# A fixed order for the beginning of the first attention in a two-layer decoder kernel

## The chip, the cores and the metric

The kernel runs on one core of a Trainium2 chip. The metric is the time of one execution on the device in microseconds (us); the median of several runs counts.

## The reference

Two decoder layers in float32 on x of 8 sequences x 512 tokens x 256 channels. Only the first attention matters here; behind it come a feed-forward layer, a second attention over another axis, and a mixture of 32 experts.

```
x = x + L0_attn(layernorm(x));  x = x + L0_ffn(layernorm(x))
x = x + L1_attn(layernorm(x));  x = x + L1_experts(layernorm(x))

L0_attn(h):                                   # 16 heads of 16 channels
  q, k, v = split_heads(h@Wq+bq), split_heads(h@Wk+bk), split_heads(h@Wv+bv)
  scores  = q.k / sqrt(48)
  pos_k   = rel_embeddings @ Wk + bk          # 128 relative positions per head
  c2p     = take(q.pos_k, bucket(i - j) + 64) # by query and distance
  p2c     = take(k.pos_k, 64 - bucket(j - i)) # by key and distance, turned
  probs   = softmax(scores + (c2p + p2c)/sqrt(48))
  return layernorm((probs.v) @ Wo + bo + h)
```

## The kernel before, in words

All tensors lie in tiles of 128 partitions. The five engines run their own queues in order; semaphores tie them. The code is written for a scheduler that may reorder what stands outside a `manual_schedule` block, and inside it keeps the written order, except that an instruction with nothing to wait for can be moved forward on its engine.

The first attention (`_l0_attention`) has three parts.

**The beginning** prepares constants. DMAs bring the weights `wk`, `wq`, `wv`, the table `relT`, bias rows, one-hot tables `oh`, and the sequences x[0] to x[7]; all but four are issued by SP, in one queue. Four scratch buffers in DRAM (`shift`, 1 MB each) are filled with zeros from the tile `zeros`. VectorE (DVE) normalises x[0] (L47 to L63: statistics, variance, a power on POOL, then one subtract-and-multiply per 128 tokens). `position_keys` (L170) makes relative keys with TensorE, adds the bias on DVE, once for all positions (`pk`) and twice for an end position broadcast (`end0`, `end1`). From `pk` and `oh` eight matmuls (L190) make the tables `posc` and `posp`. From the ends come 12 products on POOL (L205, L208), each reduced on DVE (L206, L209) into extra columns of `wq`, `wk` and the bias rows; ACT copies the bias rows (L213), POOL sets a column in each copy (L214), and 16 matmuls with one column (L217) make `bias`. POOL clears two `v` tiles (L233) and four `winc` tiles (L240). `turn` (L264) transposes normalised x[0] into `xnT`; `project` (L283) makes q and k of one group of four heads with TensorE (L291) and ACT adds the bias (L299) in four tiles `sm`.

**The strips** (L307). Scores with relative positions need each row shifted by its own index. For step u = (sequence, group, row block i, pair of heads p), TensorE multiplies q and k by the position tables (L315), ACT copies the result out (L322, `strip`), SP writes it to a `shift` buffer in DRAM (L332), and reads it back with a row step that is one element shorter (L341): once into `winp` (to be transposed later) and once into `winc`. POOL makes the part of the far positions (`own`, L325) and adds it (L352). Reads of a strip are issued after the write of the next one, additions after the strip after that. Five strips (AHEAD) are made before the first step, with the values of the first sequence (L273) between them.

**The steps**, 256 of them: TensorE makes scores (L372), with the strip five steps ahead in their midst, adds `winp` by transposing it into the same bank (L384; it needs the windows of up to two steps ahead), DVE adds `winc` and finds the maximum (L398), ACT takes the exponential (L401), TensorE transposes (L412), DVE copies (L415), TensorE weighs the values (L424). Projections and other work of the next group hang on given steps. Only the strips and steps stand in a `manual_schedule` block; the beginning is ordered by the scheduler.

Of the kernel before, what the change touches and what calls it, by code (L numbers as in the profile page):

```python
# [12 lines left out]
F32 = mybir.dt.float32  # L13
# [3 lines left out]
ALU = mybir.AluOpType  # L17
# [9 lines left out]
NG = 4  # L27
# [63 lines left out]
def _l0_attention(nc, tc, a, x, ident, mhalf, carry, prefetch):  # L91
# [6 lines left out]
    with ExitStack() as ctx:  # L98
# [16 lines left out]
        bias = wp.tile([P, 4, NG], F32, tag="bias", name="bias")  # L115
        xns = [carry.tile([P, NT, H], F32, tag=f"xn{n}", name=f"xn{n}") for n in range(3)]
        xnT = carry.tile([P, NK, S], F32, tag="xnT0", name="xnT")
        shift = [dram.tile([4 * P, 2 * W], F32, tag=f"shift{n}", name=f"shift{n}") for n in range(NSHIFT)]
        with tc.tile_pool(name="a_pos", bufs=1) as pp:
            b_rows = {n: pp.tile([P, NH, 32], F32, tag=n, name=n) for n in ("bq", "bk")}  # L120
# [16 lines left out]
            aside = wp.tile([P, 2, P], F32, tag="aside", name="aside")  # L137
            nc.sync.dma_start(aside[:, 0, :], a["later"])
            nc.sync.dma_start(aside[:, 1, :], a["earlier"])
            zeros = pp.tile([P, 2 * W], F32, tag="zeros", name="zeros")  # L140
            nc.gpsimd.memset(zeros, 0.0)
            for d in shift:
                nc.sync.dma_start(
                    d.rearrange("(q p) w -> p q w", p=P), zeros.unsqueeze(1).to_broadcast([P, 4, 2 * W])
                )
            nc.sync.dma_start(wo, a["wo_rows"].rearrange("(g p) m -> p g m", p=P))
            for name in ("bo", "ln_scale", "ln_bias"):
                nc.sync.dma_start(rows[name], a[name].partition_broadcast(P))
            for b in range(1, B):
                nc.sync.dma_start(x[b], a["x"][b].rearrange("(t p) c -> p t c", p=P))  # L150

            def normalized(pool, b):

# [9 lines left out]
                return [partial(f, t) for f in (measure, norm) for t in (0, 2)]  # L163

            ready = normalized(pp, 0)
            for n in (0, 2, 1, 3):
                ready[n]()


            def position_keys(lhsT, out):  # L170
                ps = ps_m.tile([P, S], F32, tag="misc", name="pk_ps")
# [8 lines left out]
            nc.vector.memset(pk, 0.0)  # L180
            position_keys(lambda k: relT[:, k, :], pk[:, :, :HD])
            ends = []
            for n, c in enumerate((P - 1, 0)):
                f = pp.tile([P, NH, HD], F32, tag=f"end{n}", name=f"end{n}")
                position_keys(lambda k: relT[:, k, c : c + 1].to_broadcast([P, P]), f)
                ends.append(f)
            for g in range(NG):
                for t, dst in ((0, posc), (1, posp)):
                    pe = ps_a.tile([P, S], F32, tag="psa", name="pe")
                    nc.tensor.matmul(  # L190
                        pe[:, :W], pk[:, 4 * g : 4 * g + 4, :].rearrange("p h e -> p (h e)"), oh[:, t, :], start=True, stop=True
                    )
                    if t == 0:
                        nc.vector.tensor_copy(dst[:, g, :], pe[:, :W])
                    else:
                        nc.scalar.mul(dst[:, g, :], pe[:, :W], -SCALE)
                    nc.vector.tensor_copy(dst[:, g, W - 1 : W], tail[:, t : t + 1])


            for (w, name), e0 in (((wq, "bq"), HD), ((wk, "bk"), HD + 2)):  # L200
                for n, f in enumerate(ends):
                    e = e0 + n
                    for k in range(NK):
                        prod = pp.tile([P, NH, HD], F32, tag="prod", name="prod", bufs=3)
                        nc.gpsimd.tensor_tensor(prod, w[:, k, :, :HD], f, ALU.mult)  # L205
                        nc.vector.tensor_reduce(w[:, k, :, e : e + 1].rearrange("p h e -> p (h e)"), prod, AX.X, ALU.add)  # L206
                    prod = pp.tile([P, NH, HD], F32, tag="prod", name="prod", bufs=3)
                    nc.gpsimd.tensor_tensor(prod, b_rows[name][:, :, :HD], f, ALU.mult)  # L208
                    nc.vector.tensor_reduce(b_rows[name][:, :, e : e + 1].rearrange("p h e -> p (h e)"), prod, AX.X, ALU.add)  # L209
            pb = ps_m.tile([P, S], F32, tag="misc", name="pb")  # L210
            for n, (name, e) in enumerate((("bq", HD + 2), ("bq", HD + 3), ("bk", HD), ("bk", HD + 1))):
                row = pp.tile([P, NH, 32], F32, tag=f"row{n}", name=f"row{n}")
                nc.scalar.copy(row, b_rows[name])  # L213
                nc.gpsimd.memset(row[:, :, e : e + 1], 1.0)  # L214
                for g in range(NG):
                    c = NG * n + g
                    nc.tensor.matmul(  # L217
                        pb[:, c : c + 1],
                        row[:, 4 * g : 4 * g + 4, :].rearrange("p h e -> p (h e)"),
                        ident[:, 0:1],  # L220
                        start=True,
                        stop=True,
                    )
            flat = bias.rearrange("p n g -> p (n g)")
            nc.vector.tensor_scalar(flat[:, : 2 * NG], pb[:, : 2 * NG], -SCALE, None, ALU.mult)
            nc.vector.tensor_copy(flat[:, 2 * NG :], pb[:, 2 * NG : 4 * NG])

        sb = pool("a_sb", 2)


        vs = [wp.tile([P, NT, 2, NH // 2, 2 * HD], F32, tag=f"v{n}", name=f"v{n}") for n in range(2)]
        for v in vs:
            nc.gpsimd.memset(v, 0.0)  # L233


        winc = [None] * (2 * NT)
        for p in range(2):
            for i, width in ((0, S + 2 * P), (1, S + 3 * P)):
                w = wp.tile([P, 2, width], F32, tag=f"winc{i}{p}", name="winc")
                nc.gpsimd.memset(w, 0.0)  # L240
                winc[2 * i + p], winc[2 * (NT - 1 - i) + p] = w[:, :, :S], w[:, :, width - S :]

        ctx_ps = ps_c.tile([P, S], F32, tag="ctx", name="ctx_ps")
# [9 lines left out]
        reads, adds = [], []  # L253
        cns = {b: [] for b in range(B)}
        rest = []
        now = -1

        def misc(name):

            if now < 0:  # L260
                return ps_t.tile([P, S], F32, tag="pst", name=name)
            return ps_m.tile([P, S], F32, tag="misc", name=name)

        def turn(b, k):  # L264
            pt = misc("pt")
            for t in range(NT):
                nc.tensor.transpose(pt[:, t * P : (t + 1) * P], xns[b % 3][:, t, k * P : (k + 1) * P], ident)
            evac(xnT[:, k, :], pt)

        def values(b, t):  # L270
            pv = misc("pv")
            for k in range(NK):
                nc.tensor.matmul(  # L273
                    pv[:, :H], xnT[:, k, t * P : (t + 1) * P], wv[:, k, :], start=k == 0, stop=k == NK - 1
                )
            by_head = lambda w: w.rearrange("p (h d) -> p h d", d=HD)
            for o in range(2):
                s = slice(o * H // 2, (o + 1) * H // 2)
                nc.vector.tensor_tensor(
                    vs[b % 2][:, t, o, :, HD * o : HD * o + HD], by_head(pv[:, s]), by_head(rows["bv"][:, s]), ALU.add  # L280
                )

        def project(b, g):  # L283


            def half(w, n, scale):
                if n == 0:
                    sm[b, g] = [sb.tile([P, S], F32, tag=f"sm{m}", name=f"sm{m}") for m in range(4)]
                pq = misc("pq")
                for k in range(NK):  # L290
                    nc.tensor.matmul(  # L291
                        pq,
                        w[:, k, 4 * g : 4 * g + 4, :].rearrange("p h e -> p (h e)"),
                        xnT[:, k, :],
                        start=k == 0,
                        stop=k == NK - 1,
                    )
                for m in (n, n + 1):
                    nc.scalar.activation(sm[b, g][m], pq, AF.Identity, bias=bias[:, m, g : g + 1], scale=scale)  # L299

            return [partial(half, wq, 0, -SCALE), partial(half, wk, 2, 1.0)]
# [202 lines left out]


        with tc.manual_schedule():
            for f in [partial(turn, 0, k) for k in range(NK)] + project(0, 0):
                f()
            for u in range(AHEAD):
                strips(u)  # L510
                if u:
                    values(0, u - 1)
            es, ets = None, deque()
            for now in range(len(steps) + 3):
                n = now
# [1169 lines left out]
```

## Time and profile before

| | |
|---|---|
| runs | 2081.64, 2083.9, 2084.47 us; median 2083.9 |
| profiled execution | 2102.91 us, span 2101.1 us |
| mean granted TensorE clock | 0.954 |
| busy share of the span | PE 92%, POOL 54%, DVE 66%, ACT 53% |
| DMA | 444.43 MB, mean 212 GB/s over the span |
| chain that ended last | PE 63%, DVE 11%, DMA 11%, issue 5%, POOL 5%, ACT 3% |
| first strip's write to DRAM issued | 40.46 us from the span's start |
| first score matmul of the steps | 56.49 us |

The profile is one execution on the chip. PE is TensorE, PEld its weight load, SP the queue that issues DMAs. A busy PE is not a PE at its peak: PEclk gives the clock that was granted, 1.00 being full. A matmul in float32 stands as two rows. In the first 7 us the clock column reads 1.00 only because no change of it has been recorded yet; durations of matmuls tell there. DMA share is the mean busy share of 16 DMA engines; small excesses over 1 come from the way packets are counted. In the chain of waits each piece is the work that released the next one; "issue" is time in which the engine waited for nothing that the profile shows.

### The profile page before, as it was taken

How to read it: one execution, taken by the hardware profiler on the slowest of the kernel's cores; microseconds unless marked ns; L12 is line 12 of the kernel's file. 1: busy time of each engine (PE TensorE's matmuls, PEld its weight loads, DVE VectorE, ACT ScalarE, POOL GpSimd, SP SyncE). 2: the span in 40 equal slices, each digit the busy share in tenths (PEclk: the TensorE clock that was granted, in tenths of full speed). 3: DMA queues.
4: the chain of work that ended last, by engine and by line, in shares of the span. 5: the costliest groups of instructions: out<-in, count | busy, mean ns of one | idle time of the engine just before them, and what ended most of it. 6: DMA issues, size and time to landing. Idle time of an engine off the chain costs nothing.

```text
span 2101.1 us, 49496 instructions
## 1 busy us (share of the span) xinstructions
PE 1930.6 (92%) x17956; PEld 1334.9 (64%) x17956; DVE 1389.0 (66%) x3731; ACT 1106.3 (53%) x2366; POOL 1143.3 (54%) x1340
## 2 busy tenths in 40 slices
PE   7999999999999999999889999879888778599997
PEld 4666667666666666676656666545455455388786
DVE  3677777777777777777676454257876775356666
ACT  2677777767777777677631222345433422144443
POOL 4666777767778686776733111114444443455555
PEclk7999999999999999999989999999989987699999
DMA  8999999999999999899944548601111115457888
GB/s 270 305 317 284 310 303 300 292 289 304 295 297 304 296 306 299 286 289 299 285 140 143 167 141 127 20 1 42 42 42 42 42 42 215 169 163 217 256 254 266
DMA packets 388928, 444.43 MB, mean 212 GB/s; under 512 B 43344, under 2 KB 367952, under 8 KB 388688
## 3 DMA queue, kind: packets, MB, share of 16 engines
q1 hardware_dynamic: 373904, 401.93, 63.9%
q0 software_dynamic: 13824, 38.29, 5.0%
q8 instruction: 145, 2.38, 0.5%
q10 hardware_dynamic: 960, 1.05, 0.1%
q14 instruction: 95, 0.78, 0.1%
HBM read 238.99 MB, written 202.19 MB: 210 GB/s over the span
## 4 chain that ended last, share of the span: by engine, by line
PE 63%; DVE 11%; DMA 11%; issue 5%; POOL 5%; ACT 3%; SPq 1%; another core or an unknown queue 0%; POOLq 0%; DVEq 0%; ACTq 0%
PE sc L372 7%; PE sc L384 6%; PE pge L1440 6%; PE et_ps L412 5%; PE po L684 5%; DMA winp<-shift 5%; PE ctx_ps L424 5%; PE pq L291 5%; PE ph L676 3%; PE poe L1458 3%; PE pa L315 3%; DMA shift<-strip 3%; PE pq L935 2%; PE po L460 2%; DVE prod L796 2%
## 5 line engine op out<-in xcount | busy, mean ns | idle before, releaser
L398 DVE CUSTOM_DVE_ANT_0 e<-sc,winc 128x512 f32<-128x512 f32 x512 | 333.3, 689 | 268.1 <-PE sc L384 139.4
L401 ACT ACTIVATE e<-e,low 128x512 f32<-128x512 f32 x512 | 365.7, 715 | 94.8 <-DVE low L398 93.5
L322 ACT COPY strip<-pa 128x512 f32<-128x512 f32 x512 | 275.2, 591 | 138.6 <-POOL winc L352 58.2
L325 POOL TENSOR_TENSOR own<-aside,strip 128x512 f32<-128x512 f32 x256 | 269.1, 1051 | 130.3 <-ACT strip L322 121.6
L415 DVE COPY et<-et_ps 128x512 f32<-128x512 f32 x512 | 328.5, 683 | 0.7 <-PE et_ps L412 0.7
L372 PE MATMUL sc<-sm,sm 32*128 32x256 f32 (+3 forms) x1792 | 310.5, 437 | 0.2
L315 PE MATMUL pa<-pos,sm 32*128 32x256 f32 x2048 | 297.2, 407 | 1.7 <-ACT sm L299 1.0
L879 POOL DMA_INDIRECT rows<-pay,slot x128 | 141.4, 1105 | 237.2 <-issue 224.9
L352 POOL TENSOR_TENSOR winp<-winp,own 128x256 f32<-128x256 f32 x256 | 187.3, 732 | 108.0 <-DMA winp<-shift 78.3
L372 PEld LDWEIGHTS sc<-sm,sm 32*128 32x128 f32 x1792 | 164.1, 184 | 97.0 <-DVE et L415 35.6
L384 PE MATMUL sc<-ident,winp 128*128 128x128 f32 x1280 | 204.9, 287 | 22.4 <-DMA winp<-shift 21.1
L879 POOL DMA_INDIRECT results<-y,r x160 | 157.0, 981 | 124.3 <-ACT y L1460 70.7
L352 POOL TENSOR_TENSOR winc<-winc,own 128x256 f32<-128x256 f32 x256 | 187.2, 731 | 52.2 <-DMA winc<-shift 40.6
L384 PEld LDWEIGHTS sc<-ident,winp 128*128 128x128 f32 x1280 | 137.4, 142 | 102.0 <-issue 58.3
L315 PEld LDWEIGHTS pa<-pos,sm 32*128 32x128 f32 x2048 | 178.5, 187 | 11.5 <-issue 2.0
L412 PE MATMUL et_ps<-ident,e 64*128 64x64 f32 x4096 | 184.2, 230 | 1.1 <-DVE et L415 1.1
L58 POOL TENSOR_TENSOR rstd<-var,mhalf 128x2 f32<-128x2 f32 (+1 forms) x56 | 51.1, 912 | 241.5 <-DVE var L56 208.9
L412 PEld LDWEIGHTS et_ps<-ident,e 64*128 64x128 f32 x4096 | 148.9, 140 | 44.4 <-issue 22.8
L1440 PE MATMUL pge<-store,rT 128*128 x640 | 168.0, 385 | 3.5 <-DVE rT L1434 1.1
L424 PE MATMUL ctx_ps<-et,v 128*32 128x128 f32 x4096 | 166.6, 281 | 0.5 <-DVE et L415 0.5
L291 PE MATMUL pq<-xnT,wqk 128*128 128x512 f32 x256 | 134.0, 646 | 0.1
L679 ACT ACTIVATE hT<-ph,b 128x512 f32<-128x512 f32 x64 | 44.0, 687 | 165.6 <-PE ph L676 165.5
(216 smaller groups left out, 3339.0 us busy)
## 6 DMA issues: line engine op xcount, KB each, us to landing
shift<-strip SPq DMA_DIRECT2D x256, 510.0 KB
winp<-shift SPq DMA_DIRECT2D x128, 384.0 KB
winc<-shift SPq DMA_DIRECT2D x128, 384.0 KB
winp<-shift SPq DMA_DIRECT2D x128, 256.0 KB
winc<-shift SPq DMA_DIRECT2D x128, 256.0 KB
rows<-empty SPq DMA_DIRECT2D x8, 2640.0 KB
r<-rows SPq DMA_DIRECT2D x160, 132.0 KB
z<-results SPq DMA_DIRECT2D x32, 512.0 KB
```

Of the source, the lines that this page charges most:

```text
L315: nc.tensor.matmul(pa[:, t * W : (t + 1) * W], src[rs, i * P : (i + 1) * P], pos[rs, g, :], start=True, stop=True)
L322: nc.scalar.copy(st[:, 2 * j : 2 * j + 2, :].rearrange("p t w -> p (t w)"), pas[j])
L352: nc.gpsimd.tensor_tensor(dst, dst, own[:, t], ALU.add)
L372: nc.tensor.matmul(sc[:, c0:c1], s[side_][rs, cut : cut + P], s[2 + side_][rs, c0:c1], start=c0 == 0, stop=False, skip_group_check=True,)
L384: nc.tensor.matmul(sc[:, m * P : (m + 1) * P], wins[n + 2 * (m - i)][1][:, j, (i - m + 1) * P : (i - m + 2) * P], ident, start=False, stop ...
L398: nc.vector.tensor_tensor_reduce(e, sc, wins[n][0][:, j, :], 1.0, -LOW, ALU.add, ALU.min, low)
L401: nc.scalar.activation(e, e, AF.Exp, bias=low, scale=-1.0, accum_out=totals[b, g // 2][:, i, r : r + 1])
L412: nc.tensor.transpose(bank[:, c : c + 64], e[rs, m * P : (m + 1) * P], ident[rs, rs])
L415: nc.vector.tensor_copy(et[:, f].rearrange("p j m q -> p (j m q)"), bank)
L424: nc.tensor.matmul(ctx_ps[32 * r : 32 * r + 32, i * P : (i + 1) * P], vs[b % 2][:, m, g % 2, g // 2 * 4 + r, :], et[:, :, m, :], start=m = ...
L879: ins = nc.gpsimd.indirect_dma_start(to, bass.IndirectOffsetOnAxis(ap=index, axis=0), source, None, bounds_check=last)
L1440: nc.tensor.matmul(pg[:, :H], rT[:, k * P : (k + 1) * P], w[:, k * H : (k + 1) * H], start=k == 0, stop=k == NK - 1)
```

## The change

It touches the beginning only. In words:

- The beginning is put in a `manual_schedule` block. The two end keys come before `pk`; the 12 products become a generator, `products`, whose pieces are taken between other work; normalising x[0] is taken in four pieces; all eight position tables are copied out by ACT; the constant last column of the tables is written by two DVE instructions instead of eight.
- `busy(n, zeros)` adds n matmuls of zeros by zeros, 128 x 128 by 128 x 512, into a scratch bank that nobody reads: 7 before the first keys, 5 behind `turn`, 4 before the last two bias rows: 16 in all.
- `turn` of x[0] stands before the bias matmuls; both projections of the first group stand after them.
- The six clearings (`v`, `winc`) go from POOL to DVE and stand in the code behind the projections. In the built program they stand earlier: two right after the clearing of `pk`, one after each statistics instruction of the first pair, one before the variance, one between the second and the third keys' additions.
- `zeros` grows from 512 to 2048 columns, and each `shift` buffer is cleared in rows of 8 KB instead of 2 KB. The bytes are the same.
- x[1] is loaded as before; x[2] to x[6] are issued by SP after strips 0 to 4 each, x[7] after the last of them. On SP's queue each such load stands behind a strip's write and the reads of the strip before, and ahead of the next strip's write.

```diff
+        def busy(n, w):
+            idle = misc("idle")
+            for _ in range(n):
+                nc.tensor.matmul(idle, w[:, :P], w[:, :S], start=True, stop=True)
...
-            zeros = pp.tile([P, 2 * W], F32, tag="zeros", name="zeros")
+            zeros = pp.tile([P, 8 * W], F32, tag="zeros", name="zeros")
             nc.gpsimd.memset(zeros, 0.0)
             for d in shift:
-                nc.sync.dma_start(
-                    d.rearrange("(q p) w -> p q w", p=P), zeros.unsqueeze(1).to_broadcast([P, 4, 2 * W])
-                )
+                nc.sync.dma_start(d.rearrange("(p q) w -> p (q w)", p=P), zeros)
...
-            for b in range(1, B):
-                nc.sync.dma_start(x[b], a["x"][b].rearrange("(t p) c -> p t c", p=P))
+            load(1)
...
+            def products():
+                for (w, name), e0 in (((wq, "bq"), HD), ((wk, "bk"), HD + 2)):
+                    for n, f in enumerate(ends):
+                        e = e0 + n
+                        for part in (w[:, 0], w[:, 1], b_rows[name]):
+                            prod = pp.tile([P, NH, HD], F32, tag="prod", name="prod", bufs=4)
+                            nc.gpsimd.tensor_tensor(prod, part[:, :, :HD], f, ALU.mult)
+                            nc.vector.tensor_reduce(
+                                part[:, :, e : e + 1].rearrange("p h e -> p (h e)"), prod, AX.X, ALU.add
+                            )
+                            yield
...
+            with tc.manual_schedule():
+                nc.vector.memset(pk, 0.0)
+                busy(7, zeros)
+                measure[0]()
+                for n, c in enumerate((P - 1, 0)):
+                    f = pp.tile([P, NH, HD], F32, tag=f"end{n}", name=f"end{n}")
+                    position_keys(lambda k: relT[:, k, c : c + 1].to_broadcast([P, P]), f)
+                    ends.append(f)
+                position_keys(lambda k: relT[:, k, :], pk[:, :, :HD])
+                some = products()
+                next(some)
+                norm[0]()
+                next(some)
+                measure[1]()
+                next(some)
+                norm[1]()
+                for g in range(NG):
+                    for t, dst in ((0, posc), (1, posp)):
...
+                        nc.scalar.mul(dst[:, g, :], pe[:, :W], (1.0, -SCALE)[t])
+                for t, dst in ((0, posc), (1, posp)):
+                    nc.vector.tensor_copy(
+                        dst[:, :, W - 1], tail[:, t : t + 1].to_broadcast([P, NG])
+                    )
+                for _ in range(3):
+                    next(some)
+                turn(0, 0)
+                turn(0, 1)
+                busy(5, zeros)
+                bias_columns(0, "bq", HD + 2)
+                bias_columns(1, "bq", HD + 3)
+                for _ in some:
+                    pass
+                busy(4, zeros)
+                bias_columns(2, "bk", HD)
+                bias_columns(3, "bk", HD + 1)
...
-        for v in vs:
-            nc.gpsimd.memset(v, 0.0)
...
-                nc.gpsimd.memset(w, 0.0)
+                cleared.append(w)
...
         with tc.manual_schedule():
-            for f in [partial(turn, 0, k) for k in range(NK)] + project(0, 0):
+            for f in project(0, 0):
                 f()
+            for w in cleared[2:] + cleared[:2]:
+                nc.vector.memset(w, 0.0)
             for u in range(AHEAD):
                 strips(u)
+                load(2 + u)
                 if u:
                     values(0, u - 1)
+            load(7)
```

More of the change, by code (lines that the diff above doesn't have):

```diff
@@ L117, in _l0_attention, with load, misc, turn @@
         xnT = carry.tile([P, NK, S], F32, tag="xnT0", name="xnT")
+        def load(b):
+            nc.sync.dma_start(x[b], a["x"][b].rearrange("(t p) c -> p t c", p=P))
+        def misc(name):
+            if now < 0:
+                return ps_t.tile([P, S], F32, tag="pst", name=name)
+            return ps_m.tile([P, S], F32, tag="misc", name=name)
+        def busy(n, w):
+            idle = misc("idle")
+            for _ in range(n):
+                nc.tensor.matmul(idle, w[:, :P], w[:, :S], start=True, stop=True)
+        def turn(b, k):
+            pt = misc("pt")
+            for t in range(NT):
+                nc.tensor.transpose(pt[:, t * P : (t + 1) * P], xns[b % 3][:, t, k * P : (k + 1) * P], ident)
+            evac(xnT[:, k, :], pt)
+        now = -1
         shift = [dram.tile([4 * P, 2 * W], F32, tag=f"shift{n}", name=f"shift{n}") for n in range(NSHIFT)]
@@ L165, in _l0_attention @@
             ready = normalized(pp, 0)
-            for n in (0, 2, 1, 3):
-                ready[n]()
+            measure, norm = ready[:2], ready[2:]
             def position_keys(lhsT, out):
-                ps = ps_m.tile([P, S], F32, tag="misc", name="pk_ps")
+                ps = misc("pk_ps")
                 keys = ps[:, :H].rearrange("p (h d) -> p h d", d=HD)
@@ L179, in _l0_attention @@
             pk = pp.tile([P, NH, 32], F32, tag="pk", name="pk")
-            nc.vector.memset(pk, 0.0)
-            position_keys(lambda k: relT[:, k, :], pk[:, :, :HD])
             ends = []
[L183 to L197, printed above, removed]
@@ L200, in _l0_attention @@
[L200 to L209, printed above, removed]
+            def products():
[9 more added lines that the diff above has]
+                            yield
@@ L210, in _l0_attention, with bias_columns @@
             pb = ps_m.tile([P, S], F32, tag="misc", name="pb")
-            for n, (name, e) in enumerate((("bq", HD + 2), ("bq", HD + 3), ("bk", HD), ("bk", HD + 1))):
+            def bias_columns(n, name, e):
                 row = pp.tile([P, NH, 32], F32, tag=f"row{n}", name=f"row{n}")
@@ L223, in _l0_attention @@
                     )
-            flat = bias.rearrange("p n g -> p (n g)")
-            nc.vector.tensor_scalar(flat[:, : 2 * NG], pb[:, : 2 * NG], -SCALE, None, ALU.mult)
-            nc.vector.tensor_copy(flat[:, 2 * NG :], pb[:, 2 * NG : 4 * NG])
+            with tc.manual_schedule():
[16 more added lines that the diff above has]
+                    for t, dst in ((0, posc), (1, posp)):
+                        pe = ps_a.tile([P, S], F32, tag="psa", name="pe")
+                        nc.tensor.matmul(
+                            pe[:, :W], pk[:, 4 * g : 4 * g + 4, :].rearrange("p h e -> p (h e)"), oh[:, t, :], start=True, stop=True
+                        )
[3 more added lines that the diff above has]
+                        dst[:, :, W - 1], tail[:, t : t + 1].to_broadcast([P, NG])
+                    )
+                for _ in range(3):
[10 more added lines that the diff above has]
+                bias_columns(3, "bk", HD + 1)
+                flat = bias.rearrange("p n g -> p (n g)")
+                nc.vector.tensor_scalar(flat[:, : 2 * NG], pb[:, : 2 * NG], -SCALE, None, ALU.mult)
+                nc.vector.tensor_copy(flat[:, 2 * NG :], pb[:, 2 * NG : 4 * NG])
@@ L228, in _l0_attention @@
         sb = pool("a_sb", 2)
         vs = [wp.tile([P, NT, 2, NH // 2, 2 * HD], F32, tag=f"v{n}", name=f"v{n}") for n in range(2)]
-        for v in vs:
-            nc.gpsimd.memset(v, 0.0)
-        winc = [None] * (2 * NT)
+        winc, cleared = [None] * (2 * NT), list(vs)
         for p in range(2):
@@ L255, in _l0_attention @@
         rest = []
[L256 to L268, printed above, removed]
         def values(b, t):
```

## The prediction

> **What bounds the kernel now.** The page comes first: PE is busy 92% and carries 63% of the chain, DMA 11%, and slice 1 (52.5 us) shows a clock of 0.7. The change touches only the start of the first attention: from the score matmuls of step 0 on, both built programs hold the same instructions in the same order on every engine. So I cut the start into stretches. First three of 5 us (columns: length, busy time and instructions of each engine, clock, DMA share, GB/s):
>
> ```profile
> 20.00:25.00 5.00, 2.18 (x5) 0.49 (x4) 2.40 (x9) 1.52 (x3) 5.00 (x7) 0.92 0.96 235
> 25.00:30.00 5.00, 4.51 (x16) 3.46 (x16) 1.40 (x4) 1.14 (x2) 4.88 (x9) 0.50 1.04 254
> 30.00:35.00 5.00, 5.00 (x19) 3.97 (x19) 0.00 (x0) 0.00 (x0) 0.00 (x0) 0.50 1.09 350
> ```
>
> TensorE works at half clock, POOL is full until 30, DMA is full. Then the stretches from the bias to the first strip's write, from there to the first score matmul, and on to the first long wait:
>
> ```profile
> 36.00:40.46 4.46, 2.88 (x10) 1.51 (x11) 0.16 (x2) 3.50 (x6) 0.00 (x0) 0.50 0.38 134
> 40.46:56.50 16.04, 16.04 (x50) 9.46 (x48) 1.46 (x6) 4.30 (x8) 7.57 (x9) 0.50 0.77 234
> 56.50:87.30 30.80, 28.93 (x374) 20.12 (x374) 21.99 (x58) 23.91 (x54) 21.68 (x27) 0.97 1.01 322
> ```
>
> The strips are TensorE at half clock with DMA only 0.77 busy; from 56.5 on DMA is full and TensorE nearly so. The chain (start, length, what) says where that ends:
>
> ```profile
> 29.93 6.24 issue
> 36.17 0.70 ACT sm L299
> 36.91 2.43 PE pa L315 x8
> ...
> 82.35 4.91 DMA winp<-shift
> 87.26 0.04 issue
> 87.30 0.55 PE sc L384 x3
> ```
>
> At 87.3 a step waits for a window that came 4.91 us after its issue: a backlog of DMA ends last there. Everything after starts from this wait in the same order, so **what moves the end is when DMA reaches this window**. Rows for prices (timeline):
>
> ```profile
> 13.89 3.29 DVE L63 TENSOR_SCALAR xn<-x,mv,rstd 128x256 f32<-128x256 f32 x2 [0.42 <-POOL rstd L58]
> 17.73 1.03 PE L190 MATMUL pe<-oh,pk 128*128 128x256 f32 x4
> 32.47 3.41 PE L217 MATMUL pb<-ident,row 128*128 128x1 f32 x16
> 42.45 2.08 PE L273 MATMUL pv<-wv,xnT 128*128 128x256 f32 x4
> 57.11 0.73 POOL L352 TENSOR_TENSOR winp<-winp,own 128x256 f32<-128x256 f32 x1 [0.21 <-DMA winp<-shift]
> ```
>
> Two matmuls of 256 columns take 1.03 at full clock and 2.08 at half; a filler of 512 columns is worth as much (two of that shape run in 1.72 in the chain at 59.1: 0.86 each in a row). All sums are in the time of the profiled execution (span 2101.1, 2102.9 with what lies around it); the runs' median of 2083.9 is 0.9% lower, so a few us carry over as they are.
>
> **Clearings.** POOL loses six memsets: 1.80 x 2 + 1.38 + 1.60 + 1.39 + 1.60 = 9.6 us. DVE gets them, in the built order among its first 15 instructions although the code has them after the projections. DVE shows one memset: 0.48 for 512 columns. Straight by columns (10752) six cost 10.1 us; with the 0.16 that stays when copies of 256 and 512 columns (0.42, 0.68) are extrapolated to none, 7.7. I take 8. Cover: DVE waits 4.89 us for x[0] until 6.28, and in the new order has only one pair of statistics before the first keys' addition at 12.4. Five clearings fit there even at the dearer price (after 6.28: three of 5376 columns 5.0, statistics 1.1, so 12.4); without that cover it would be that 5 us. The sixth (1.4, at most 1.9) stands between the second and third keys' additions and is on the path.
>
> **Fillers, first seven.** They wait for the clearing of zeros, now 2048 columns: 0.92 + 1.80 = 2.7. The keys, which began at 6.99 at half clock, stand behind them. In the trace clock and work fit so: keys from 6.99 ran at 2.04 and 2.08 a pair, full speed came near 13.5, some 6 us later. With 5 us at half (3 fillers) and four at 0.86: end at 11.3; never lifted, 2.8 + 7 x 2.06 = 17.2. I take 11.3; keys 1.1, addition 0.42: first ends row at 12.7 (12.08 before), the second 13.4 (17.5 before), clearing 1.4, third addition at 15.3.
>
> **DVE and POOL after that.** The fixed order puts on DVE: reduce 0.42, two normalisings 0.8, reduce 0.42, statistics 1.3: variance at 18.2, then the power on POOL, 0.72: 19.0. The four products behind it on POOL wait for it, from 14.1 on. They end at 19.0 + 4 x 0.74 = 22.0. The second normalising pair falls beside them; with POOL occupied such a pair took 3.29, alone 0.8, so 21.1 to 23, and three reduces behind it end between 22.9 and 24.5: take 23.5. Row copies on ACT 1.14, the clearings of row columns on POOL behind them, only then the six k products: 24.8 + 6 x 0.74 = 29.3, reduce 0.42, row copies 1.14, column 0.14: 31.0. Position tables (eight matmuls of 0.5 and evictions of 0.38 over two banks, about 1.1 a pair with the handing over: 4.5 us from 15.3) and transposes hide beside this; the nine other fillers (7.7 us at full clock) end near 31 to 32.6, so up to 1.5 is theirs. Eight bias matmuls 1.7 at full (half of 3.41): 33.5. Then the projections, which ran before and between the bias rows, now follow: 2 x 1.8 = 3.6: 37.1, last activations 38.3. **Before: 36.17 + 2.42 = 38.6.** So I put no gain and no loss on the front: TensorE's 10.4 us at half clock (25.5 to 35.9) is gone, but the chain over DVE, POOL and ACT that takes its place is as long. Range: -3 (fillers and normalising beside, bias sums smaller) to +4 (clock lost in a gap, 3.6 of projections doubled).
>
> The Trainium skill, TensorE: Matmul & The Clock Gate, Part 1, says about 3.4 us of sustained work lift the clock and an idle window of that length drops it. The trace does not show it so: TensorE is busy all of 40.46 to 56.5 at 0.50. By the rule the fillers would end near 10.5 and the forecast be 0.8 us lower; by the row, where such work does not lift the clock, it stands as it is, or the strips stay at 4 us, still beside a full DMA.
>
> **Strips.** At full clock a strip with its values costs 2 us, not 4; ACT 1.07, POOL 1.05 + 1.46 = 2.5, so POOL sets 2.5 and DMA more: 0.51 MB written and 0.51 to 0.77 read, at 322 GB/s 3.2 to 4 us. TensorE is no longer last, DMA is.
>
> **Zeros in 8 KB rows.** The same 4.2 MB; with 2 KB rows they run at 383 to 388 GB/s between 12 and 20 us, all landed 15 us before the first strip. Price zero. The Trainium skill, DMA: Bandwidth & Descriptors, speaks against a gain too: line rate from 512 B on; at its ceiling of 435 GB/s an estimate of 1.3 us, hidden.
>
> **Loads.** x[2] to x[7], 6 x 0.524 = 3.1 MB, ran until about 37 in the shade of the half-clock TensorE; now each stands on SP between two strips' writes, ahead of the next write and window reads in the same queue. At 350 GB/s (30:35) they cost 9.0 us. Room: from 40.46 to 87.3 DMA was busy 16.04 x 0.77 + 30.8 = 43.2 us, idle 3.7. With the loads 52.2: the window of 87.3 comes at 40.5 + 52.2 = 92.7, **5.4 us later** if no gap is left. Cheaper in the gaps (halved by their own latency): +3; at 322 GB/s (9.8): +6.1. The DMA that now idles from about 28 to 40 is what pays. Later absorption: DMA shares stay 0.93 to 1.00 in every 50 us to 1000, and the steps after follow one another, so I expect none.
>
> Sum: front 0, loads +5.4, the rest 0: 2083.9 + 5.3 = **2089**; own range 2086 to 2092.
>
> **Rivals.** *Faster, the strips' half clock:* the first score waited on TensorE (58.44) 0.6 us after its window was ready. If the front ends 8 us early (products back to back: 12 x 0.74 from 12.7, rows, bias, projections: about 31), strips start at 32 and the window of 87.3 comes at 32 + 52 = 84: 2080.5 (down to 2077). It decides once the first strip is written before 35. For: 9.6 us of clearings leave POOL. Against: variance and row waits above. 0.17. *No change:* front 2 to 3 early and loads partly in gaps (+3 to +5): within 4 us of 2084; 0.25. *The fillers don't do what they say:* the clock stays low on zeros, or drops in the gaps at 13 to 15 and 19 to 22 (a gap of 3.2 us before 25.5 cost it): keys at 17, fillers 18 us at half: front +5 to +10, so 2093 to 2100. 0.15. *Forecast:* 0.43.
>
> **Numbers.** 0.2% is 4.2 us, about what a measurement of this kernel can tell from none. Slower by more: 0.15 and most of 0.43: 0.56. Within: 0.25 and a little of it: 0.27. Faster: 0.17. The range leaves out the half of the faster case below 2080 and of the low clock above 2096.
>
> **What would show it.** Right: first strip copy near 39 to 40; DMA share under 0.5 from 28 to 39 and 1.0 from 42 to past 90; the window reads of strip 2 land near 58, not before 54; full clock in the strips. Wrong: the first strip before 35, DMA idle after 45, or keys beginning near 7.

## The result, and the profile after

| | before | changed |
|---|---|---|
| median of 5 runs each, same chip | 2083.9 us (2079.99 to 2088.38) | 2094.13 us (2091.5 to 2101.34) |
| ratio | | 1.0057, 95% interval 1.0031 to 1.0082 |
| profiled execution | 2102.91 us, span 2101.1 | 2091.5 us, span 2089.6 |
| first strip's write issued | 40.46 us | 40.46 us |
| wait of step 8 for its window ends | 87.30 us | 90.40 us |
| bytes moved from 36 to 100 us | 17.87 MB | 19.93 MB |

The change makes the kernel slower by about half a per cent in this comparison; two repeats on two different chips, among the experiments, gave 1.0018 (its interval holds 1) and 1.0038. The median of 2094.13 lies above the forecast of 2089 and 2.1 us above the prediction's own range of 2086 to 2092. The two profiled executions stand the other way round than the medians, because single executions of one program drift apart by several us in the long attention loop: the changed kernel's is 1.4 us behind the other at the start of step 10, level at step 120 and 8 us ahead at step 255. So their spans can't be compared, and the readings below stay in the first 110 us.

The stretches of the changed kernel, for the same cuts as before (length, busy time and instructions of PE, PEld, DVE, ACT and POOL, clock, DMA share, GB/s):

```profile
25.00:30.00 5.00, 5.00 (x25) 3.25 (x24) 2.53 (x6) 0.70 (x2) 3.83 (x7) 1.00 0.50 138
30.00:35.00 5.00, 5.00 (x25) 3.17 (x24) 0.24 (x2) 0.43 (x1) 0.23 (x2) 1.00 0.01 3
...
40.46:56.50 16.04, 16.04 (x53) 9.64 (x56) 1.95 (x8) 4.35 (x8) 8.14 (x9) 0.53 0.98 316
56.50:87.30 30.80, 28.89 (x354) 19.12 (x352) 19.92 (x53) 21.66 (x49) 18.72 (x23) 0.91 1.03 342
```

TensorE's clock is now full from 25 until the first strip (it was 0.50), and DMA stands still from 30 until then, where before it ran at 350 GB/s from 30 to 35. In the strips DMA is full (0.98, it was 0.77), and TensorE is back at half clock, 0.53. The chain of the changed kernel (start, length, what) shows what ends last there:

```profile
50.91 6.14 DMA shift<-strip
...
57.11 6.33 DMA winp<-shift
...
85.73 4.62 DMA winp<-shift
90.36 0.04 issue
90.40 0.55 PE sc L413 x3
```

Before, the chain had no wait for DMA from the first strip until 82.35; now it waits for a strip's write and then for its window already at 51, before the steps begin. The last three lines are the step that waited until 87.30 before. The DMA view of 36 to 100 us names what is new in the queue (transfers and KB each), first before:

```profile
DMA packets 16060, 17.87 MB, mean 279 GB/s; under 512 B 697, under 2 KB 16051, under 8 KB 16051
...
shift<-strip SPq DMA_DIRECT2D x16, 510.0 KB
```

then in the changed kernel:

```profile
DMA packets 18293, 19.93 MB, mean 311 GB/s; under 512 B 751, under 2 KB 18285, under 8 KB 18285
...
shift<-strip SPq DMA_DIRECT2D x15, 510.0 KB
x<-in_x SPq DMA_DIRECT2D x6, 512.0 KB
```

There are one strip write fewer than before and six loads of x more.

### The profile page after: what moved, and what is told of

The parts are those of the page before. It is cut to its first block, busy times and chain, and to the rows that moved or that the text cites. A ratio compares the mean times of both kernels' runs of the same rounds, so it can differ in the third digit from the quotient of the medians.

```text
span 2089.6 us, 49560 instructions
## 1 busy us (share of the span) xinstructions
PE 1935.6 (93%) x17988; PEld 1334.0 (64%) x17988; DVE 1390.5 (67%) x3727; ACT 1106.5 (53%) x2370; POOL 1135.5 (54%) x1334
## 4 chain that ended last, share of the span: by engine, by line
PE 62%; DMA 12%; DVE 11%; POOL 6%; issue 5%; ACT 4%; SPq 0%; another core or an unknown queue 0%; POOLq 0%; ACTq 0%; DVEq 0%
PE sc L401 7%; PE pge L1473 6%; DMA winp<-shift 6%; PE sc L413 5%; PE po L717 5%; PE et_ps L441 5%; PE pq L320 5%; PE ctx_ps L453 4%; PE poe L1491 3%; PE ph L709 3%; PE pa L344 2%; DMA winc<-shift 2%; DMA shift<-strip 2%; PE pq L968 2%; ACT strip L351 2%
## 5 line engine op out<-in xcount | busy, mean ns | idle before, releaser
L320 PE MATMUL pq<-xnT,wqk 128*128 128x512 f32 x256 | 129.5, 630 | 0.0
```

## The experiments

Two theories. **L:** the loads between the strips are what the change costs, since DMA sets the pace there. **F:** the front decides (the fixed order, the fillers, and the clock that falls again in the strips), and the loads are hidden. Each group of four ran on one chip together with the kernel before. "Step 8" and "step 10" are the starts of those steps' first maximum on DVE (the custom operation that makes `e` from `sc` and `winc`) in the profiled execution; before they were at 87.9 and 99.3, and 91.0 and 100.7 in the first profile of the changed kernel. The kernel before has only this one profile, none beside the three groups. The ratios are those of the record; the quotients of the medians differ a little from them.

| run | loads of x | first strip written | step 8 | step 10 | ratio to before, 95% interval |
|---|---|---|---|---|---|
| e1_after: changed kernel again | between | 40.70 | 93.2 | 103.0 | 1.0018 (0.9998 to 1.0038) |
| e2_front: changed, loads ahead | ahead | 40.16 | 87.0 | 96.7 | 1.0004 (0.9980 to 1.0027) |
| e3_between: before, loads between | between | 39.88 | 93.3 | 103.0 | 1.0017 (0.9999 to 1.0036) |
| e4_nofill: changed, no zero matmuls | between | 36.90 | 90.1 | 101.5 | 1.0025 (1.0005 to 1.0045) |
| e5_double: each load made twice | between | 40.52 | 119.2 | 130.6 | 1.0157 (1.0121 to 1.0192) |
| e6_early: e2 and e4 together | ahead | 37.10 | 86.2 | 95.9 | 0.9998 (0.9974 to 1.0022) |
| e7_hold: e6, filler in each strip | ahead | 38.91 | 86.9 | 96.6 | 1.0016 (0.9994 to 1.0038) |
| e8_rows: before, zeros in 8 KB rows | ahead | 41.55 | 91.0 | 100.7 | 1.0010 (0.9987 to 1.0034) |
| e9_more: changed, six more transfers | between | 40.32 | 101.8 | 111.5 | 1.0070 (1.0044 to 1.0096) |
| e10_pool: changed, clearings on POOL | between | 43.28 | 96.5 | 106.2 | 1.0041 (1.0023 to 1.0059) |
| e11_after: changed kernel again | between | 40.44 | 95.2 | 106.5 | 1.0038 (1.0023 to 1.0053) |
| e12_front: e2 again | ahead | 40.19 | 87.3 | 98.7 | 1.0002 (0.9985 to 1.0018) |

**The changed kernel again.** No edit; it is what the other three of its group are held against.

> The changed kernel once more, beside the three below on the same chip, so that they can be compared with it. Theory L (loads: the six loads of x between the strips are what the change costs, since DMA is the last to be ready from the first strip on) and theory F (front: the fixed order, the fillers and the clock cost it) both expect what was measured: 1.003 to 1.008 of the kernel before, 2090 to 2099 us.

It is 4.5 us above before (2081.17 against 2076.7), ratio 1.0018: less than both theories expected, and no clear loss by itself, since the interval holds 1. The strips look as in the first profile, with longer waits: 7.82 us for the strip's write at 54.56, 8.13 us for its window at 62.44.

**The loads alone, undone and done.** In the changed kernel, all loads go ahead of the strips again:

```
-            load(1)
+            for b in range(1, B):
+                load(b)
...
-                load(2 + u)
...
-            load(7)
```

> The changed kernel with all seven loads of x up front again, as before; every other queue is as in the changed kernel. L: 5 to 10 us less than the changed kernel, so 2084 to 2089; in the profile the first strip's write stays near 40.5, DMA is busy until about 37, and the step that came at 91.0 (ninth maximum on VectorE) comes near 86. F: no more than 2 us less than the changed kernel.

And the reverse in the kernel before: x[2] to x[7] between the strips, nothing else.

```
-            for b in range(1, B):
-                nc.sync.dma_start(x[b], a["x"][b].rearrange("(t p) c -> p t c", p=P))
+            load(1)
...
                 strips(u)
+                load(2 + u)
...
+            load(7)
```

> The kernel before with one edit: x[2] to x[7] are loaded between the strips as in the changed kernel; only SP's queue differs. L: slower than before by 4 to 9 us (2088 to 2093), DMA idle from about 30 to 40 and full from 45 to past 90. F: within 2 us of before (2084).

Undone, the loss goes: step 8 at 87.0, and the median 2078.82 is 2.4 us below that of the changed kernel beside it. Done alone, it comes: step 8 at 93.3, with none of the rest of the change, and a median 4.6 us above before (2081.33 against 2076.7). The chain of the kernel before with the loads between:

```profile
55.16 6.80 DMA shift<-strip
...
63.79 8.17 DMA shift<-strip
...
71.97 5.58 DMA winp<-shift
```

These are the waits of the changed kernel, and not those of before, whose chain had its first DMA wait at 82.35. It speaks for L. The time alone did not settle it yet: L had forecast 5 to 10 us for the loads undone, F at most 2, and 2.4 is hardly more than that; the intervals of the ratios of e1, e2 and e3 overlap, and that of e3 holds 1.

**The front without fillers.**

```
-                busy(7, zeros)
...
-                busy(5, zeros)
...
-                busy(4, zeros)
```

Without them the first projection also moves ahead of the bias columns on TensorE.

> The changed kernel without the 16 matmuls of zeros; without them the scheduler also moves the first projection ahead of the bias rows on TensorE. L: the loads still cost theirs; the first keys begin at 7 instead of 11 but at half clock, the projection of q is off the path: first strip's write 0 to 4 us earlier than 40.46, and 2089 to 2094. F: back within 3 us of before (2081 to 2087).

The first strip was written at 36.90, 3.6 us earlier than with fillers, but step 8 began at 90.1, only 0.9 before the earliest of the changed kernel's three (91.0, 93.2, 95.2), and the ratio is no better than that of e1. F's forecast, a median within 3 us of before, failed: it is 5.3 us above (2081.98 against 2076.7). So the sixteen zero matmuls and the place of the projection behind the bias columns delay the first strip, and the delay is hidden: with the strips earlier, the chain waits 8.36 us for a strip's write at 60.66.

**The loads doubled.**

```
                 load(2 + u)
+                load(2 + u)
...
             load(7)
+            load(7)
```

> The changed kernel with each of the six loads between strips made twice (the same data to the same place); nothing else differs. Theory L (the loads between the strips are what the change costs, because DMA sets the pace there): another 3.1 MB, at 350 to 385 GB/s 8.2 to 9.0 us, so the first maximum of step 10 at 109 to 113 (103.0 in the repeat of the changed kernel, 100.7 in its first profile), and the median 4 to 9 us above that of the changed kernel repeated (2081.2), some 0.4 to 0.6% over before. Rival F (the front, the fillers and the clock in the strips set the time and the loads are hidden): step 10 at 101 to 104, the median within 2 us of the changed kernel's.

This missed both forecasts: 27.6 us later at step 10 and 29 us in the ratios (1.0157 against 1.0018). The edit did more than it meant. The second load writes the same tile as the first, and SP holds it back, with everything on its queue behind it. SP's instructions in the timeline (start, length):

```profile
48.84 6.37 SPq L120 DMA_DIRECT2D x<-in_x  x2
55.25 0.51 SPq L361 DMA_DIRECT2D shift<-strip  x1
```

Two issues that otherwise take 0.5 us each take 6.4 together, and the next strip's write stands behind them. In e9 below, where the second transfer of each pair has another destination, the issues of a pair take 1.3 to 3.2; so it is the shared tile, most likely a wait for the first load to land. The run prices a load together with this wait (27.6 / 6 = 4.6 us per load), not the bytes alone. It shows one thing more: a delay of this size at step 10 is still there at the end.

**The early front with the loads ahead.** The edits of e2 and e4 together.

> The changed kernel without the sixteen zero matmuls and with all loads of x ahead of the strips: the two single experiments together. Without the zero matmuls alone the first strip was written at 36.90 instead of 40.46, but nothing came of it. Theory L: with the loads gone from between the strips the earlier strip counts, so the first maximum of step 10 comes at 92 to 96 (96.7 with the loads in front alone, 99.3 before), and the median is 2 to 5 us below before. Rival F (the clock in the strips sets the pace): with the loads in front the strips run at half clock from the first on and the 3.6 us are lost again; step 10 at 96 to 100, the median within 2 us of before. Third: the loads in front now run into the writes of the first strip, which come earlier, and step 10 is at 97 to 101.

Step 10 at 95.9 is in L's range, but only 0.8 us before e2's 96.7 (on another chip) although the first strip came 3.1 us sooner, and the median is that of before. So the early front is worth next to nothing by step 10 even with the loads out of the way, as far as one profile of each can tell. L's forecast for the median (2 to 5 us below before) failed.

**Holding the clock in the strips.** To e6 is added:

```
                 strips(u)
+                busy(1, xnT[:, 0, :])
```

> The kernel of e6_early with one more matmul of 128 rows and 512 columns (its result unused) behind each of the five first strips. It asks why the strips run at half clock although TensorE is busy: if the 32-row position matmuls don't count enough for the clock and 128-row ones do, a third of TensorE's time more in 128-row matmuls lifts it, pa and pv go from 2.08 to 1.03 us a pair, and the five strips take 5 x 2.9 = 15 us of TensorE in place of 5 x 4.1 = 20; step 10 then 0 to 4 us earlier than in e6_early. If it isn't lifted, the five extra matmuls cost 5 x 2.06 = 10 us of TensorE in the strips; step 10 up to 10 us later than in e6_early, less what DMA hides. Theory L says DMA hides part of either, so the difference to e6_early is smaller than TensorE's own.

TensorE's matmuls in the timeline of this kernel (one filler is recorded as two matmuls):

```profile
39.67 2.08 PE L342 MATMUL pa<-pos,sm 32*128 32x256 f32 x8
41.68 2.08 PE L132 MATMUL idle<-xnT 128*128 128x512 f32 x2
...
48.59 1.13 PE L342 MATMUL pa<-pos,sm 32*128 32x256 f32 x8
49.66 1.13 PE L132 MATMUL idle<-xnT 128*128 128x512 f32 x2
50.62 1.03 PE L300 MATMUL pv<-wv,xnT 128*128 128x256 f32 x4
```

The clock comes back at 45.88, 8 us after the first of the added matmuls, and stays full (in e6 it was half until 57.30); a strip with its values and one matmul more then takes 3.0 us of TensorE instead of 4.0. The first strip is written 1.8 us later than in e6, but not because of the added matmuls, the first of which runs at 37.67: in this execution the clock was at half from 28.8 to 32.2, and the second projection took 3.46 us, 1.95 in e6. TensorE ends the fifth strip's share at 54.6 against 53.2, and step 10 is at 96.6 against 95.9, where 0 to 4 us earlier was expected. From the first strip's write to step 10 it is 57.7 us against 58.8. So it answers the question on the clock, but is no clean test of F: the two started apart, and a gain of 1.1 us is within the scatter.

**The zeros in 8 KB rows alone,** in the kernel before.

```
-            zeros = pp.tile([P, 2 * W], F32, tag="zeros", name="zeros")
+            zeros = pp.tile([P, 8 * W], F32, tag="zeros", name="zeros")
...
-                nc.sync.dma_start(
-                    d.rearrange("(q p) w -> p q w", p=P), zeros.unsqueeze(1).to_broadcast([P, 4, 2 * W])
-                )
+                nc.sync.dma_start(d.rearrange("(p q) w -> p (q w)", p=P), zeros)
```

> The kernel before with one part of the change alone: the zeros of the shift buffers written in rows of 8 KB from a zeroed tile four times as wide. The prediction gave it no price: the same 4.2 MB, landed 15 us before the first strip's write, and one clearing on POOL longer by 1.3 us. L and F: the first strip's write 0 to 1.4 us later than 40.46, step 10 within 2 us of before's 99.3, the median within 2 us of before. If rows of 8 KB moved much faster, the zeros' stretch between 12 and 20 us would show over 400 GB/s and the loads behind them would end 1 to 3 us earlier.

As expected, the first strip's write comes 1.1 us later and the ratio's interval holds 1. Between 12 and 20 us the transfers ran at 422 GB/s (421 in the changed kernel), where before it was 385: the long rows are some 10% faster there, and nothing waits for it. Step 8 was 3.1 us later than before with no load between the strips, as much as in the changed kernel's first profile; so a step's start in one execution is good to some 2 or 3 us only, and the groups have to be read together.

**More bytes, without a wait.** Six copies of the same blocks to places in DRAM that nothing reads, one behind each load.

```
+        spare = [dram.tile([P, NT, H], F32, tag=f"spare{n}", name=f"spare{n}") for n in range(6)]
+
+        def again(n):
+            nc.sync.dma_start(spare[n], a["x"][2 + n].rearrange("(t p) c -> p t c", p=P))
...
                 load(2 + u)
+                again(u)
...
             load(7)
+            again(5)
```

> The changed kernel with six more transfers between the strips, one behind each load of x, that copy the same 0.524 MB blocks to places in DRAM that nothing reads; no instruction waits for them, so that, unlike the doubled loads, nothing on the queue is held up by a transfer that has not ended. Theory L: 3.1 MB more at 350 to 385 GB/s is 8.2 to 9.0 us of DMA (up to twice that if a copy inside DRAM costs double), so step 10 begins at 108 to 118 (100.7 and 103.0 in the two profiles of the changed kernel), and the median is 4 to 15 us above that of the changed kernel on the same chip. Rival F: the loads are hidden, step 10 at 100 to 104, the median within 2 us of the changed kernel's.

On the same chip as the next three: 5.1 us above the changed kernel in the median (2105.71 against 2100.62), 5.0 us later at step 10 (111.5 against 106.5). Bytes between the strips cost time, which speaks against F's "within 2 us"; the intervals of the two ratios still overlap (1.0044 to 1.0096 and 1.0023 to 1.0053). The first strip's write that the chain waits for took 9.73 us, against 5.76 in the changed kernel beside it. Held against the mean step 10 of the three changed kernels (103.4), it is 8.1 us later.

**The clearings on POOL again,** in the changed kernel.

```
             for w in cleared[2:] + cleared[:2]:
-                nc.vector.memset(w, 0.0)
+                nc.gpsimd.memset(w, 0.0)
```

> The changed kernel with the six clearings on POOL again, in the places that the scheduler gives them: four between the first power and the products, two between the products and the row clearings. The prediction put them on DVE at 8 us of work that is covered but for 1.4 us. On POOL they cost 9.6 us by the rows of before. If POOL carries the front's chain (power, products, row clearings, first strip at 40.46), the first strip's write comes at 44 to 50, less the 1.4 us that DVE saves, step 0 at 61 to 66 and step 10 at 103 to 110; the median 2 to 8 us above the changed kernel's. If POOL's clearings fit into its waits, the first strip comes at 39 to 41 and the median is the same.

The first strip comes 2.8 us later than with DVE's clearings, at 43.28, between the two branches of the expectation (39 to 41, and 44 to 50). It does not reach the time: 2099.4 against 2100.62.

**The changed kernel and its loads ahead, once more.** These two decide, since they ran side by side with the narrowest intervals.

> The changed kernel a third time, beside before on the chip of the other three: the two measures so far are 1.0057 and 1.0018. Theory L: some 3 to 8 us slower than before, ratio 1.001 to 1.004; step 10 at 100 to 104. A ratio under 0.999 would speak against a loss.

> The changed kernel with all loads of x ahead of the strips, a second time, beside the changed kernel on the same chip. Theory L: the loads between the strips are the loss, so it is 2 to 6 us below the changed kernel and within 3 us of before; step 10 at 95 to 98. Rival F: the same time as the changed kernel within 2 us.

The changed kernel is slower than before (1.0023 to 1.0053); with nothing altered but the place of six loads on SP's queue it isn't (0.9985 to 1.0018). The two intervals don't meet, and the medians are 7.7 us apart (2100.62, 2092.89). Both are beyond L's sizes (2 to 6 us in the median; step 10 at 106.5 and 98.7, forecast at 100 to 104 and 95 to 98). The stretches that show it, first the changed kernel, then the one with its loads ahead:

```profile
30.00:35.00 5.00, 5.00 (x25) 3.15 (x24) 0.24 (x2) 0.42 (x1) 0.21 (x2) 1.00 0.01 3
...
40.46:56.50 16.04, 16.04 (x53) 9.69 (x56) 1.95 (x8) 4.30 (x8) 8.08 (x9) 0.53 0.99 311
```

```profile
30.00:35.00 5.00, 5.00 (x25) 3.31 (x24) 0.24 (x2) 0.27 (x1) 0.13 (x1) 1.00 1.05 344
...
40.46:56.50 16.04, 16.04 (x52) 9.46 (x54) 1.96 (x8) 4.39 (x8) 8.06 (x10) 0.51 0.83 248
```

TensorE, DVE, ACT and POOL do the same work in both. DMA is busy at 30 to 35 in one and idle in the other, and pays for it in the strips. The waits for DMA in the chains: with the loads between,

```profile
46.78 5.76 DMA shift<-strip
...
52.61 5.70 DMA winp<-shift
```

and with the loads ahead the first is

```profile
76.29 4.42 DMA shift<-strip
80.80 5.93 DMA winp<-shift
```

No version beat the kernel before: the best, e6, is at 0.9998 (0.9974 to 1.0022), which is no difference. All these runs put the extra transfers on the same queue, ahead of a strip's write; none separates their bytes from their place in it, by another queue for instance.

## Why the prediction was right, step by step

**What bounds it: right.** A wait for a window on a full DMA queue ended last in the strips, and moving bytes in and out of that stretch moved the time (e2, e3, e9, e12), while moving POOL's work and the first strip's write by 3 us either way did not (e4, e6, e10).

**Clearings: right in place, dear by a little.** The memsets on DVE:

```profile
7.01 1.34 DVE L539 MEMSET winc<- 128x1536 f32 x1 [0.27 <-issue]
...
9.02 1.55 DVE L539 MEMSET winc<- 128x1792 f32 x1 [0.32 <-issue]
...
10.99 1.76 DVE L539 MEMSET v<- 128x2048 f32 x1 [0.38 <-issue]
```

By the rows six are 9.3 us, where 8 were taken from bounds of 7.7 and 10.1. But each stands behind idle time marked issue that grows with its size (0.27, 0.32, 0.37 to 0.38 us), and with that the six take 11.2, above both bounds. Five ended at 12.75 beside the seven fillers, and the first keys' addition began at 12.68, so they were just about covered. The sixth stood in front of the third addition, as foreseen, and kept DVE from 13.43 to 15.48: 2.05 us, where 1.4, at most 1.9, was taken.

**Fillers, DVE and POOL: right but for the split.** The points of the front, as forecast and as the trace has them: fillers end 11.3, 11.22; second ends row 13.4, 13.43; third 15.3, 15.84; variance 18.2, 18.25; the products of q end 22.0, 22.13; those of k 29.3 (with reduce and row copies still to come), 28.81; bias columns end 33.5, 34.28; projections end 37.1, 37.82; last activation ends 38.3, 39.13. The first strip's write came at 40.46 as before: the last activation ended 0.5 us later than before, and the first position matmuls made up for it at full clock (1.55 us, 2.38 before). That the two agree to the hundredth is chance. What took the place of TensorE's half clock is not only the chain over DVE, POOL and ACT. It ends at the same time without the fillers (products of k at 29.04 in e4, row columns set at 30.83; 28.81 and 30.62 here), and yet e4's first strip comes 3.6 us sooner: there the bias columns end at 32.33, here at 34.28, behind the last four fillers, and the projections come only after them. So some 2 us of fillers, taken as up to 1.5, and the place of the projections fill the rest. The rival *the fillers don't do what they say* was half true: zeros lift the clock (full from 7.19), but it was at half again from 17.43 to 20.84, after TensorE had waited 1.62 us ahead of the position tables and was busy for only 0.38 us from 14 to 16. The first strip shows no cost of it.

**Strips: the clock was wrong, and nothing hung on it.** "At full clock a strip with its values costs 2 us" failed: half clock from 41.32 to 58.39, and a strip with its values took 4. The prediction had allowed for it ("the strips stay at 4 us, still beside a full DMA"). It did not matter, because in the changed kernel's strips the DMA share is 0.98 at that half clock already: DMA was last without TensorE's getting faster. No run here has the strips at full clock for nothing, so what that would be worth with the loads ahead, where the share is 0.83, is open.

**Zeros: right in time** (e8), though not for the rate: 8 KB rows did run faster (421 and 422 GB/s against 385).

**Loads: right mechanism, right size within the scatter.** The forecast put step 8's window at 92.7. The changed kernel's three profiles have it at 90.40, 92.67 and 94.63, in the mean 92.6; with the loads ahead it came at 86.45 and 86.77. That the mean comes so near is partly luck, since single profiles scatter by 2 to 3 us (e8). In the medians the loads cost 2.4 (e1 against e2), 7.7 (e11 against e12) and 3.5 us (e3's ratio), where 5.4 was said, and the first comparison gave 10.2. The room of 3.7 us of idle DMA was used up: the share of 56.5 to 87.3 is 1.03. Where the sum is rough is in more of the same: e9's further 3.1 MB, which at 350 to 385 GB/s should cost 8.2 to 9.0 with no room left, cost 5.0.

**No later absorption: not shown.** e11 is 7.8 us behind e12 at step 10, 9.4 behind at step 120, 7.7 in the median. But e3 and e4, 6.3 and 4.8 us behind e2 at step 10, are only 0.3 and 0.4 behind at step 120, and their profiled executions end within 1 us of e2's (spans 2073.4, 2074.4 and 2073.4); e1 is 6.2 behind e2 at step 10 and 2.9 at step 120. So a lag of this size can shrink in the loop, which fits the small differences of that group's medians; what takes it up is open. Nor does a lead last: being 2 to 3 us early at step 10 (e2, e6, e7) left no mark on the median. The first measure, 1.0057, is more than the mean of the repeats; why executions of one program differ by 6 us at step 10 (100.7, 103.0, 106.5) stays open.

Of the marks named beforehand, the first strip copy (39.33), the DMA shares (0.03 from 28 to 39, 1.03 from 42 to 92) and the window of strip 2 near 58 (POOL's addition to it began at 58.01, as soon as it had landed) came; full clock in the strips did not.

## What to carry to other kernels

Before moving a transfer to "where it is needed", look in the windows for the DMA share at both places: here it left a stretch of 10 us with a share of 0.01 for one that became full, and 3.1 MB cost 2 to 8 us. A stretch in which one engine looks slow (TensorE at half clock in the strips) can hide a second limit right below it; filling the second's slack can then be a loss. Hold the changed kernel, the undone part and the part alone against each other on one chip, and repeat the pair that decides, because single profiles differ by more than the effect.

## What the hardware showed that was not expected

**A busy TensorE at half clock.** In the strips it is busy all the time (16.04 of 16.04 us) at 0.53 and does not speed up until the steps begin. The strips alternate matmuls of 32 rows and of 128, 2.08 us each; one more 128-row matmul per strip lifted the clock some 8 us after the first of them (e7). That 32-row matmuls count for less in what the clock follows fits this, but no run tests it by itself. The Trainium skill, TensorE: Matmul & The Clock Gate, Part 1, has one busy window of about 3.4 us lift it; the fillers of zeros agree (full 4.4 us after their first), the strips don't.

**DVE stands still behind POOL's clearings.** With the clearings on POOL, the timeline shows

```profile
14.12 2.91 POOL L539 MEMSET winc<- 128x1536 f32 x2
...
14.64 2.85 DVE L63 TENSOR_SCALAR xn<-x,mv,rstd 128x256 f32<-128x256 f32 x2
...
22.14 4.19 DVE L254 COPY pos<-tail 128x4 f32<-128x4 f32 x2
...
22.75 3.54 POOL L539 MEMSET v<- 128x2048 f32 x2
```

In the changed kernel the same pair of normalisings took 0.73 and the copies of 128 x 4 elements 0.70. Here the copies last until POOL's memsets end (22.14 + 4.19 = 26.33, 22.75 + 3.54 = 26.29), and the normalisings end less than 0.5 us after theirs (17.49, 17.03). The Trainium skill, SBUF — State Buffer, SBUF: two separate sides, describes a pair of ports that DVE and POOL share as an exclusive lock, held for a whole instruction; this agrees with it.

**A load of a tile on top of another load** holds the issuing queue, 5.2 to 7.0 us for the two issues in e5, and with it every later transfer of that queue.
